# Selective scan: the weighting by C one unit later, in front of the scan

## The chip, the cores and the metric

The kernel runs on one core of a Trainium2 chip. A core has five engines that work through queues of their own, each in order, and that wait for one another through semaphores: TensorE (PE in the profile; its weight loads are PEld), VectorE (DVE), ScalarE (ACT), GpSimd (POOL) and SyncE (SP), which here only issues DMAs. The metric is the device time of one execution in microseconds. The kernel before takes 7552.04 us, the median of three runs (7550.52 to 7557.68).

## The reference

The program is two layers on an image `x` of 2 batches, 128 channels and 64 x 64 places: a deformable convolution with an expert FFN (layer 0), and a Mamba-like mixer with another expert FFN (layer 1). The change touches the selective scan inside the mixer. Per batch it runs over 4096 places with 256 channels and 16 states each:

```python
dA = jnp.exp(jnp.einsum('bdl,dn->lbdn', delta, A))
dBu = jnp.einsum('bdl,bnl,bdl->lbdn', delta, Bm, x)
def step(s, inp):
    a, bu, c = inp
    s = a * s + bu
    return (s, jnp.einsum('bdn,bn->bd', s, c))
_, ys = lax.scan(step, zeros, (dA, dBu, Ct))
y = jnp.transpose(ys, (1, 2, 0))
y = y + x * D[None, :, None]
y = y * silu(z)
out = jnp.einsum('md,bdl->blm', out_proj_w, y)
```

The state of each channel and state number is a running sum over places; at each place the 16 states are weighted by C and added up, x times D is added, the sum is gated by `silu(z)` and projected.

## The kernel before, in words

The scan (`L1Conv.scan`, from line 1568) cuts the work into 512 **units**: 2 batches x 8 pieces of 512 places x 2 halves of the channels x 16 states. A unit has 128 channels on the partitions and 512 places along the row. For unit u the steps are:

- `fetch` (L1615, SyncE): the row of B, broadcast over the partitions, into `bcb`, six units ahead.
- `drive` (L1597, GpSimd): `db` = delta x u times B, three units ahead.
- `decay` (L1604, ScalarE): `da` = exp(delta times A), two units ahead; two slots, so `da` of unit u+2 needs scan(u) finished.
- the scan itself (L1685, VectorE): `h`, 128 x 512; then GpSimd copies the last place into `state` (L1694). Three slots.
- `turn` (L1623, TensorE): four transposes of `h` into `ht` in PSUM, so that the places lie on the partitions. They run in the helper `transpose4`, line 120. Two slots: `ht` of unit u-1 needs that `ht` of unit u-3 has been weighted.
- `weigh` (L1631 on VectorE, L1633 on ScalarE): `w` = `ht` times C, which is now one number per partition. VectorE does all four quarters while there is side work of batch 1 left, later two, and one in batch 1; ScalarE does the others, and its part waits for VectorE's part of the same unit. Four slots.
- `add` (L1639, L1642, TensorE): four transposes back that add `w` onto `py` in PSUM.
- `gate` (L1654, VectorE), once per half: `py` times `zz`, the gated input.

`add` and `gate` wait in a list, `adds`, with the number of the unit in which `flush` issues them.

The order of the work is the order in which the Python loop issues it: every engine's queue holds it in that order. Unit u of the loop issues: DMAs, scan(u), drive(u+3), the state copy, decay(u+2), turn(u-1), weigh(u-2), the adds that are due, and then **other work**. This other work comes from generators that yield after each small step. `side` is the preparation of the next piece (`prepare`, L1484: the taps L1461 or L1434, `px` L1517, `xd` L1520, `ct` L1530, the softplus chain L1540 to L1561 with `e` and `q`) and the projection of the last one (`project`, L1718: matmuls L1727, the residual L1737, its store L1738); it takes two steps per unit. `rest`, only while batch 0 is scanned, is all that batch 1 still has ahead of its own scan: the fuse convolution (L892), the expert FFN of layer 0 in 8 groups (`px` L1045, `ws` L1052, the router L1000 to L1027, `pg` L1032, `po` L1058 and L1061, `xt` L1080) and the patch convolutions (L1251, L1264, L1286, with reductions L1304, L1306, L1343 and L1344 on VectorE). It is paced by a credit of one per unit.

Of the kernel before, what the change touches and what calls it, by code (L numbers as in the profile page):

```python
# [117 lines left out]
def transpose4(nc, ident, ps, srcs):  # L118
    for j, s in enumerate(srcs):
        nc.tensor.transpose(ps[:, j, :], s, ident)  # L120
# [1011 lines left out]
class L1Conv:  # L1132
# [435 lines left out]
    def scan(self, sp, ps, pp, rest, ahead):  # L1568


        env, nc = self.env, self.env.nc
        states = [sp.tile([P, 2, DS], F32, name=f"state{b}", bufs=1) for b in range(B)]
        for state in states:
            nc.vector.memset(state, 0.0)

        dg = sp.tile([P, 2, P], F32, name="dg", bufs=1)
        for h in range(2):
            nc.vector.tensor_scalar(dg[:, h, :], env.ident, self.D[:, h : h + 1], None, ALU.mult)
        NK = N // LC

        def nxt(k):

            res = {}
            return self.prepare(k // NK, k % NK, sp, pp, res), res

        gen, res = nxt(0)
        for _ in gen:
            pass
        units = [(k, half, n) for k in range(B * NK) for half in range(2) for n in range(DS)]
        pieces, das, dbs, rows, hs, hts, ws = {0: res}, {}, {}, {}, {}, {}, {}  # L1590

        def drive(u):

            if u < len(units):
                k, half, n = units[u]
                dbs[u] = sp.tile([P, LC], F32, name="db", bufs=AHEAD + 1)
                nc.gpsimd.tensor_tensor(dbs[u], pieces[k]["du"][:, half, :], rows.pop(u), ALU.mult)  # L1597

        def decay(u):
            if u < len(units):  # L1600
                k, half, n = units[u]
                das[u] = ps.tile([P, LC], F32, name="da")
                dl = pieces[k]["dl"][:, half, :]
                nc.scalar.activation(das[u], dl, AF.Exp, scale=self.A[:, half, n : n + 1])  # L1604

        fetched = 0

        def fetch(u):
            nonlocal fetched
            while fetched <= min(u, len(units) - 1):  # L1610
                k, half, n = units[fetched]
                if "bc" not in pieces.get(k, {}):
                    break
                rows[fetched] = sp.tile([P, LC], F32, name="bcb", bufs=BCB)
                nc.sync.dma_start(out=rows[fetched], in_=pieces[k]["bc"][n].partition_broadcast(P))  # L1615
                fetched += 1

        adds, py = deque(), {}

        def turn(u):  # L1620
            hts[u] = ps.tile([P, GT, P], F32, name="ht")
            h = hs.pop(u)
            transpose4(nc, env.ident, hts[u], [h[:, j * P : (j + 1) * P] for j in range(GT)])  # L1623

        def weigh(u):
            k, half, n = units[u]
            ct, ht = pieces[k]["ct"], hts.pop(u)
            ws[u] = sp.tile([P, GT, P], F32, name="w", bufs=4)
            cut = GT if rest.todo else 2 if k < NK else 1
            by = ct[:, 0:cut, n : n + 1].to_broadcast([P, cut, P])  # L1630
            nc.vector.tensor_tensor(ws[u][:, 0:cut, :], ht[:, 0:cut, :], by, ALU.mult)  # L1631
            for j in range(cut, GT):
                nc.scalar.activation(ws[u][:, j, :], ht[:, j, :], AF.Copy, scale=ct[:, j, n : n + 1])  # L1633

        def add(u):
            k, half, n = units[u]
            if n == 0:
                py[k] = ps.tile([P, LC], F32, name="py", bufs=1)
                nc.tensor.matmul(py[k], dg[:, half, :], pieces[k]["xs"][:, half, :], start=True, stop=False)  # L1639
            w = ws.pop(u)  # L1640
            for j in range(GT):
                nc.tensor.matmul(  # L1642
                    py[k][:, j * P : (j + 1) * P],
                    w[:, j, :],
                    env.ident,
                    is_transpose=True,
                    start=False,
                    stop=n == DS - 1 and j == GT - 1,
                )

        def gate(u):
            k, half, n = units[u]
            y = pieces[k]["zz"][:, half, :]
            nc.vector.tensor_tensor(y, y, py.pop(k), ALU.mult)  # L1654

        def project(k):
            return self.project(k // NK, k % NK, pieces[k]["zz"], sp, pp)

        def flush(u):
            while adds and adds[0][0] <= u:  # L1660
                adds[0][1](adds.popleft()[2])

        fetch(BCB - 3)
        for u in range(AHEAD):
            drive(u)
        decay(0)
        decay(1)
        side, keep, credit = Side(), None, 0
        for u, (k, half, n) in enumerate(units):
            state = states[k // NK]  # L1670
            if k and half == 0 and n == 5:
                side.todo.appendleft(project(k - 1))
            last = n == DS - 4 and half == 1
            if last and k == NK - 1:
                rest.drain()

            if k + 1 < B * NK and k + 1 not in pieces and (k != NK - 1 or not rest.todo):
                gen, pieces[k + 1] = nxt(k + 1)
                side.add(gen)
            fetch(u + BCB - 2)  # L1680
            if k >= NK and u % 24 == 12:
                ahead()

            hs[u] = sp.tile([P, LC], F32, name="h", bufs=3)
            nc.vector.tensor_tensor_scan(  # L1685
                hs[u], das.pop(u), dbs.pop(u), state[:, half, n : n + 1], ALU.mult, ALU.add
            )
            if last:
                side.drain()
                fetch(u + BCB - 2)  # L1690
            drive(u + AHEAD)

            if keep:
                nc.gpsimd.tensor_copy(*keep)  # L1694
            keep = state[:, half, n : n + 1], hs[u][:, LC - 1 : LC]
            decay(u + 2)
            if u:
                turn(u - 1)
            if u > 1:
                weigh(u - 2)  # L1700
            flush(u)
            adds.append((u + (4 if n == 0 else 3), add, u))
            if n == DS - 1:
                adds.append((u + 4, gate, u))

            for _ in range(2 if rest.todo or k != NK - 1 else 4):
                side.step()
            credit += 1
            while credit > 0 and rest.todo:
                credit -= rest.step()  # L1710
        turn(u)
        weigh(u - 1)
        weigh(u)
        flush(u + 4)
        for _ in project(B * NK - 1):
            pass

# [50 lines left out]
class L1Ffn:  # L1768
# [16 lines left out]
    def ahead(self):  # L1785

        if self.early is None:
            self.early = self.ctx.enter_context(self.env.tc.tile_pool(name="f1x", bufs=EARLY, side="right"))
        if len(self.w1) < EARLY:
            self.fetch(self.early)  # L1790
# [325 lines left out]
```

## Time and profile before

| what | value |
|---|---|
| median of three runs | 7552.04 us |
| the profiled execution | 7555.38 us, its span 7553.5 us |
| mean granted TensorE clock | 0.825 |
| busy: PE, DVE, ACT, POOL | 5203.1, 5857.3, 2135.7, 5036.0 us |
| first and last scan (L1685) start | 5764.7 and 7299.4 us |
| scans: count and mean | 512 of 1273 ns |

The scan phase is the last fifth of the program but for the closing FFN of layer 1. In the page's 40 slices it fills numbers 31 to 39. All times in the views are counted from the start of the span. A group's row gives the busy time, the mean of one instruction, and after the bar the idle time of its engine just before it with what ended that idle time.

### The profile page before, as it was taken

The page shows a single profiled execution, that of the slowest core. Times are in us where ns is not written, and L with a number is a line of the kernel's source. Part 1 is how long each engine was busy: PE and PEld are TensorE (multiplying, and loading weights), DVE is VectorE, ACT ScalarE, POOL GpSimd, SP SyncE. Part 2 cuts the span into 40 slices and gives each one's busy share as a digit, 9 for nine tenths or more (in the row PEclk, how much of TensorE's full clock was granted, in tenths as well). Part 3 has the DMA queues.
Part 4 walks back from the last instruction along what each step waited for, and adds up shares of the span by engine and source line. Part 5 has one row for each costly group of instructions (what it writes and reads, how often), then busy time and mean ns, then how long its engine had stood idle before and what let it go on. Part 6 is the DMA issues. An engine that isn't in the chain of part 4 may idle for free.

```text
span 7553.5 us, 71416 instructions
## 1 busy us (share of the span) xinstructions
PE 5203.1 (69%) x22497; PEld 3269.2 (43%) x22497; DVE 5857.3 (78%) x6710; ACT 2135.7 (28%) x4194; POOL 5036.0 (67%) x5062
## 2 busy tenths in 40 slices
PE   4666777777767675766666766666556788867668
PEld 3344444444444442333323444434223567755444
DVE  6878888888888887788888877777775787678782
ACT  2211111111111111311111121211114675667870
POOL 4666777777777777777777776677775445567850
PEclk7887887878888887888888887877777898888899
DMA  7886777776777767877777777687775334555444
GB/s 239 253 275 206 216 210 218 211 220 208 220 213 219 214 210 251 281 232 212 224 217 216 217 232 235 207 251 216 228 208 188 118 103 129 138 155 163 153 148 156
DMA packets 667316, 1550.02 MB, mean 205 GB/s; under 512 B 181668, under 2 KB 230988, under 8 KB 666940
## 3 DMA queue, kind: packets, MB, share of 16 engines
q0 software_dynamic: 307200, 1006.88, 44.2%
q1 hardware_dynamic: 332540, 492.98, 20.9%
q10 hardware_dynamic: 27200, 45.59, 1.6%
q8 instruction: 182, 2.98, 0.2%
q14 instruction: 194, 1.59, 0.1%
HBM read 1436.70 MB, written 110.84 MB: 205 GB/s over the span
## 4 chain that ended last, share of the span: by engine, by line
PE 39%; issue 18%; another core or an unknown queue 13%; DVE 8%; POOL 7%; ACT 7%; DMA 3%; SPq 1%; ACTq 0%; DVEq 0%; POOLq 0%
PE out L816 17%; PE pst L120 6%; POOL v L748 5%; PE po L437 4%; POOL db L1597 2%; DVE h L1685 2%; ACT st L796 2%; DVE v L789 2%; PE ps L1264 2%; PE pfo L892 1%; PE ps L1251 1%; PE px L1045 1%; PE ht L120 1%; DVE q L1557 1%
## 5 line engine op out<-in xcount | busy, mean ns | idle before, releaser
L748 POOL DMA_INDIRECT v<-table,idx x3840 | 4042.1, 1053 | 1629.6 <-issue 1047.7
L789 DVE TENSOR_TENSOR v<-v,pw 128x2048 f32<-128x2048 f32 x960 | 2192.0, 2283 | 611.3 <-DMA v<-table,idx 429.3
L816 PE MATMUL out<-st,regw 128*128 128x512 f32 x3840 | 2234.7, 708 | 225.3 <-issue 164.1
L796 ACT COPY st<-pst 128x512 f32<-128x512 f32 x960 | 556.9, 586 | 4402.2 <-remote 2198.4
L120 PE MATMUL pst<-ident,v 128*128 128x128 f32 x3840 | 721.3, 313 | 1061.0 <-issue 874.3
L791 DVE TENSOR_TENSOR v<-v 128x1024 f32<-128x1024 f32 x960 | 1177.3, 1226 | 33.0
L816 PEld LDWEIGHTS out<-st,regw 128*128 128x128 f32 x3840 | 790.7, 228 | 887.1 <-issue 813.5
L120 PEld LDWEIGHTS pst<-ident,v 128*128 128x128 f32 x3840 | 517.3, 161 | 1431.5 <-issue 1214.8
L1597 POOL TENSOR_TENSOR db<-du,bcb 128x512 f32<-128x512 f32 x512 | 670.9, 1311 | 493.5 <-DVE h L1685 382.8
L1685 DVE TENSOR_TENSOR_SCAN h<-da,state,db 128x512 f32<-128x512 f32 x512 | 651.8, 1273 | 77.9 <-ACT da L1604 48.0
L792 DVE TENSOR_TENSOR v<-v 128x512 f32<-128x512 f32 x960 | 664.2, 692 | 33.0
L120 PE MATMUL ht<-ident,h 128*128 128x128 f32 x2048 | 357.6, 303 | 221.0 <-ACT w L1633 150.9
L437 PE MATMUL po<-wa,win 128*128 128x147 f32 x2112 | 386.4, 306 | 104.7 <-issue 101.9
L437 PEld LDWEIGHTS po<-wa,win 128*128 128x128 f32 x2112 | 339.4, 204 | 226.6 <-issue 226.2
L1604 ACT ACTIVATE da<-delta,w_A_log 128x512 f32<-128x512 f32 x512 | 357.7, 699 | 262.6 <-DVE h L1685 258.0
L120 PEld LDWEIGHTS ht<-ident,h 128*128 128x128 f32 x2048 | 259.8, 155 | 345.4 <-ACT w L1633 223.0
L1631 DVE TENSOR_TENSOR w<-ht,ct 128x128 f32<-128x128 f32 (+2 forms) x512 | 232.8, 455 | 181.9 <-PE ht L120 179.8
L1251 PE MATMUL ps<-ipw,hs 128*120 128x128 f32 x1408 | 212.9, 309 | 181.7 <-ACT X L1198 92.8
L1642 PE MATMUL py<-ident,w 128*128 128x128 f32 x2048 | 337.2, 295 | 0.0
L1251 PEld LDWEIGHTS ps<-ipw,hs 128*120 128x120 f32 x1408 | 196.3, 212 | 235.9 <-ACT X L1198 109.7
L1642 PEld LDWEIGHTS py<-ident,w 128*128 128x128 f32 x2048 | 272.4, 155 | 23.3 <-issue 23.0
L1264 PE MATMUL ps<-tm,X 120*88 120x48 f32 x2048 | 214.9, 278 | 87.2 <-ACT Y L1198 42.2
(327 smaller groups left out, 5289.5 us busy)
## 6 DMA issues: line engine op xcount, KB each, us to landing
bcb<-bc SPq DMA_DIRECT2D x512, 256.0 KB
regw<-in_regw SPq DMA_DIRECT2D x192, 640.0 KB
v<-table,idx POOLq DMA_INDIRECT x3840
yd<-ys ACTq DMA_DIRECT2D x128, 256.0 KB
yc<-yd SPq DMA_DIRECT2D x16, 2048.0 KB
wt<-in_weight SPq DMA_DIRECT2D x32, 1024.0 KB
tm<-pos SPq DMA_DIRECT2D x32, 720.0 KB
pos<-zero SPq DMA_DIRECT2D x48, 240.0 KB
```

What stands on the lines that cost most here:

```text
L120: nc.tensor.transpose(ps[:, j, :], s, ident)
L437: m()
L748: self.env.nc.gpsimd.indirect_dma_start(out=v[:, j, :], out_offset=None, in_=self.table[b], in_offset=bass.IndirectOffsetOnAxis(ap=idx[:, ...
L789: nc.vector.tensor_tensor(v4, v4, w, ALU.mult)
L791: nc.vector.tensor_tensor(up, up, v4[:, :, 2:4, :], ALU.add)
L792: nc.vector.tensor_tensor(v4[:, :, 0, :], v4[:, :, 0, :], v4[:, :, 1, :], ALU.add)
L796: nc.scalar.copy(st, pt.rearrange("p j t -> p (j t)"))
L816: nc.tensor.matmul(self.out[half], self.regw[t // CH][:, t % CH, half * P : (half + 1) * P], st, start=first, stop=last,)
L1251: nc.tensor.matmul(ps[:, k, :], patch, own[o], start=True, stop=True)
L1597: nc.gpsimd.tensor_tensor(dbs[u], pieces[k]["du"][:, half, :], rows.pop(u), ALU.mult)
L1642: nc.tensor.matmul(py[k][:, j * P : (j + 1) * P], w[:, j, :], env.ident, is_transpose=True, start=False, stop=n == DS - 1 and j == GT - 1,)
L1685: nc.vector.tensor_tensor_scan(hs[u], das.pop(u), dbs.pop(u), state[:, half, n : n + 1], ALU.mult, ALU.add)
```

## The change

`weigh` leaves its place behind `turn` and moves to the front of the loop's body, ahead of the scan, for a unit one lower: unit u now issues weigh(u-3), scan(u), and so on, with the other work of the unit still at the end. The unit numbers in `adds` grow by one. The three last units are weighted behind the loop.

```diff
             if k >= NK and u % 24 == 12:
                 ahead()
 
+            if u > 2:
+                weigh(u - 3)
             hs[u] = sp.tile([P, LC], F32, name="h", bufs=3)
             nc.vector.tensor_tensor_scan(
                 hs[u], das.pop(u), dbs.pop(u), state[:, half, n : n + 1], ALU.mult, ALU.add
@@ -1696,12 +1698,10 @@
             decay(u + 2)
             if u:
                 turn(u - 1)
-            if u > 1:
-                weigh(u - 2)
             flush(u)
-            adds.append((u + (4 if n == 0 else 3), add, u))
+            adds.append((u + (5 if n == 0 else 4), add, u))
             if n == DS - 1:
-                adds.append((u + 4, gate, u))
+                adds.append((u + 5, gate, u))
 
@@ -1709,9 +1709,9 @@
         turn(u)
-        weigh(u - 1)
-        weigh(u)
-        flush(u + 4)
+        for i in range(u - 2, u + 1):
+            weigh(i)
+        flush(u + 5)
         for _ in project(B * NK - 1):
             pass
```

## The prediction, as it was put on record

> **What bounds the kernel now.** The profiled execution took 7555.4 us (span 7553.5); the median of the three runs is 7552.0, so it lies 3.3 us above. I read the groups first, to see what one unit costs:
>
> ```profile
> L1685 DVE TENSOR_TENSOR_SCAN h<-da,state,db 128x512 f32<-128x512 f32 x512 | 651.8, 1273 | 77.9 <-ACT da L1604 48.0
> L120 PE MATMUL ht<-ident,h 128*128 128x128 f32 x2048 | 357.6, 303 | 221.0 <-ACT w L1633 150.9
> L1631 DVE TENSOR_TENSOR w<-ht,ct 128x128 f32<-128x128 f32 (+2 forms) x512 | 232.8, 455 | 181.9 <-PE ht L120 179.8
> L1604 ACT ACTIVATE da<-delta,w_A_log 128x512 f32<-128x512 f32 x512 | 357.7, 699 | 262.6 <-DVE h L1685 258.0
> ```
>
> The third line is the change's target: VectorE stands still 180 us in front of `w`, waiting for the transposes `ht`. The scan runs from 5765 to 7300 us only; all before it is untouched. Next came the busy time by stage (PE, PEld, DVE, ACT, POOL; beside it the fuse convolution, the FFN, the patch convolutions, the change of batch, then batch 1 alone):
>
> ```profile
> 5765.00:5893.00 128.00, 100.55 (x424) 57.98 (x424) 91.63 (x132) 96.03 (x134) 70.60 (x86) 0.91 0.60 210
> 5893.00:6200.00 307.00, 245.13 (x1236) 168.34 (x1237) 245.44 (x489) 210.90 (x423) 127.91 (x152) 0.85 0.29 91
> 6200.00:6666.00 466.00, 384.38 (x3087) 344.32 (x3086) 333.28 (x355) 263.56 (x448) 249.24 (x303) 0.86 0.53 143
> 6666.00:6740.00 74.00, 52.76 (x278) 37.74 (x276) 55.75 (x69) 52.80 (x113) 50.57 (x65) 0.79 0.41 131
> 6740.00:7300.00 560.00, 406.23 (x2399) 299.00 (x2400) 449.07 (x586) 461.69 (x1139) 452.13 (x567) 0.86 0.49 158
> ```
>
> TensorE is busiest in the convolutions (384 of 466 us); in the FFN it and VectorE are equal (245 of 307); with batch 1 alone VectorE, ScalarE and GpSimd are level at 80 to 82%, each waiting in turn for another. So no stage is one engine's, and what counts is which wait is lengthened.
>
> **What moves.** Call R the other work that a unit issues. VectorE's order is now scan(u), w(u-2), R(u), scan(u+1), w(u-1); it becomes scan(u), R(u), w(u-2), scan(u+1). That is a rotation: where R is empty nothing moves. In the timeline VectorE has an R in 181 of the 512 units; in the other 331 its order stays. GpSimd's and SyncE's queues keep their order, but SyncE's DMAs after L1738 wait for R. On ScalarE the part of `w` done there passes R too. On TensorE each `add` moves one unit back; the `add` matmuls (L1642) waited 0.0 us, slots of `w` (4) stay as far apart, and gating follows its last `add` by one unit as before: at nothing. If that cover went, one `add` (4 x 0.11 us issue) would show. The tail gains one `add`, 0.4 us.
>
> Three things follow from the rotation.
>
> (a) **Stalls filled.** Where `w` now waits for `ht` and an R stands behind it, R fills the wait, at most min(wait, R). Going through the timeline unit by unit: 47 of 133 stalls have an R behind them. The overlaps sum by stage to 3.7 (fuse), 0.7 (FFN), 19.7 (convolutions), 2.1, and 8.7 us (batch 1). The clearest:
>
> ```profile
> 6900.40 0.29 DVE L1631 TENSOR_TENSOR w<-ht,ct 128x128 f32<-128x128 f32 x1 [1.07 <-PE ht L120]
> 6900.60 0.68 DVE L1737 TENSOR_TENSOR xr<-xr,po 128x512 f32<-128x512 f32 x1
> 6901.31 0.32 SPq L1738 DMA_DIRECT2D x<-xr  x1
> 6902.20 0.41 SPq L1504 DMA_DIRECT2D zc<-zsd  x1
> ```
>
> L1737 (0.68 us) waits behind a `w` that waits 1.07 us, and SyncE's queue behind L1738: in front of `w` it ends some 0.7 us earlier, and the loads behind L1738 with it. This recurs in all 8 pieces of batch 1: -5.5 us, which I take whole. In the convolutions I take half (-10), since TensorE, which VectorE awaits there, is the fuller engine; of the fuse stage half (-2).
>
> (b) **Waits uncovered.** Where R itself waits, `w` stood in front of it and cost nothing; behind it, it adds its 0.67 us (0.27 in batch 1). The sums of min(w, wait of R) are 1.5, 12.3, 3.4, 1.1 and 4.7 us. The FFN's:
>
> ```profile
> 6058.68 1.28 DVE L1685 TENSOR_TENSOR_SCAN h<-da,state,db 128x512 f32<-128x512 f32 x1
> 6059.29 0.60 PE L120 MATMUL ht<-ident,h 128*128 128x128 f32 x4
> 6059.87 0.67 DVE L1631 TENSOR_TENSOR w<-ht,ct 128x512 f32<-128x512 f32 x1
> 6061.95 1.02 PE L1045 MATMUL px<-ew,xnt 128*128 128x512 f32 x2
> 6063.01 0.69 DVE L1052 TENSOR_TENSOR ws<-px,gate 128x512 f32<-128x512 f32 x1 [1.69 <-PE px L1045]
> ```
>
> `w` ends at 6060.5, then L1052 waits 1.69 us for `px`. Some such matmuls themselves wait for an R that now comes 0.67 us sooner, so I take 7 of 12.3 in the FFN, 3 of the convolutions' 3.4, 1 at the change of batch; batch 1's is within (d).
>
> (c) **TensorE held longer.** `ht(u-1)` needs the slot that w(u-3) frees. That `w` used to stand before R(u-1), and now stands behind it, right before scan(u). So I compared the start of every `ht(u-1)` with that of scan(u): in 65 units TensorE was there first, by 3.7, 37.2, 57.3, 11.7 and 25.1 us in sum. Behind a held `ht` stand its `add` and the unit's own matmuls. Not all of it is lost, since TensorE often waits later anyway. Worked through: `ht` at 6051.71 would start near 6053.7, and pushes L1639, L1642, L1058, two L1061 groups and `px` 2.0 us back, onto the L1052 above: 2.0 lost. The group from 5991.02 idles 2.58 us before L1032 and loses 0.2; that from 6147.95 idles 5.72 there and loses about 0.5. Eight such groups at about 1: +8. In the convolutions four bursts of VectorE (at 6267, 6303, 6540, 6640 us) hold it 5.9 to 10.7 us each, mostly idle before as well: 2, 0.7, 1.8 and 1: +5.5.
>
> (d) **ScalarE in batch 1.** Its part of `w` (three copies, 0.88 us) falls behind `xd`, which waits for `px`:
>
> ```profile
> 6924.28 0.91 ACT L1633 ACTIVATE w<-ht,ct 128x128 f32<-128x128 f32 x3
> 6926.88 0.58 ACT L1520 COPY xd<-px 40x512 f32<-40x512 f32 x1 [1.69 <-PE px L1517]
> 6935.56 1.43 DVE L1547 TENSOR_SCALAR q<-e 128x1024 f32<-128x1024 f32 x1 [0.71 <-ACT e L1545]
> ```
>
> Then come the 0.88 us of `w`, da, `ht`, `pt`, `ct`, all in one row up to `e`, for which VectorE already waits 0.71 us: about +1.1 a piece, 8.8 in all. After the q chain (L1547 to L1561) one more `ht` and `add` remain to be done before the chain of scans goes on, about 0.5 a piece: +4.
>
> Sum by stage: fuse -2; FFN +7 +8 = +15; convolutions -10 +3 +5.5 = -1.5; change of batch +1; batch 1 -5.5 +8.8 +4 = +7; tail +0.4. Together **+20 us**: 7575.4 for the profiled execution, and **7572** against the median. Bounds: all of (a) and nothing else, -35 (7517); all uncovered waits (23.0), 15 groups and bursts at the dearest 2.0 us (30) and 1.8 a piece in batch 1 (14), +67 (7619).
>
> A rule bears on (c), apart from this sum. Rows first: the four `ht` took 0.60 us at 6059.29 but 1.11 us at 6922.48 after 6.39 us of idling, and the 16 L1061 took 1.97 us at 6055.02 but 3.67 at 5996.00. The Trainium skill, "TensorE: Matmul & The Clock Gate", Part 1, says that an idle window of some 3.4 us halves TensorE's clock until it has been busy as long; each wait that newly passes that length would cost about 1.7 us (an estimate from that page). Ten of the 65 holds in (c) are that long, so by the rule the sum would be about 17 us higher; I leave it out, since TensorE idled near most of them before.
>
> **The rivals.**
>
> *Faster.* The circle scan, da, ScalarE's copies, TensorE's matmuls, `ht`, `w`, scan in the convolutions may be bound by its latency and not by TensorE. Then all 19.7 us of overlap there are gained, and what (c) and (d) hold back is made up for: -2 -20 -5.5 +7 (FFN, uncovered waits) = -20, 7532. It decides if the convolutions' 96 us of waits of `w` fall below about 80 with the stage shorter by as much. For it: 59 of the 133 stalls lie there. Against: TensorE is 82% busy and most of those stalls (64 of 96 us) have no R behind them. Chance 0.14.
>
> *No change.* From R to R the interval holds one scan and one `w` in both orders; if the moved waits all cancel, the time stays within 15 us (0.2% of 7552, about what a measurement of this kernel can tell from no change). That is also the case in which the change doesn't do what it says, since 331 units keep their order. 7552, chance 0.26.
>
> *Much slower.* The halved clock or longer holds raise (c) to its bound: about 7600. Chance 0.12, beside 0.48 for my own case; together 0.60 for slower.
>
> The range: below 7538 lie the faster cases (0.14), above 7604 about 0.07.
>
> **What would show it.** Right: waits of `w` for `ht` fall from 180 us by 30 to 60 and the total still doesn't fall; waits of `ht` for `w` on VectorE grow (10.4 us in the FFN, 33.1 in the convolutions now); the FFN stage is the longer by 10 to 20 us; L1737 no longer stands behind a stalled `w`; in batch 1 `q` waits longer for `e` than 0.71 us. Wrong: the FFN stage keeps its 307 us, or the convolutions lose more than 10. What would overturn the prediction most is (c): if TensorE's held matmuls are made up for everywhere, the time is 7552 or less.

## The result, and the profile after

The changed kernel took 7578.24 us (median of 8 runs, 7570.08 to 7599.68) against 7552.87 us (7543.96 to 7562.25) for the kernel before in the same rounds: the ratio is 1.003 with a 95% interval of 1.0021 to 1.0038, so it is slower by some 25 us. The execution that was profiled took 7599.68 us (span 7597.9), the longest of the eight, 21 us above the median. So its stage times overstate the loss: the five stages below come to 38 us more than before, and another 6.5 us lie ahead of the first scan, where the two programs are the same.

The groups of after, which answer to the four shown of before:

```profile
L1687 DVE TENSOR_TENSOR_SCAN h<-da,state,db 128x512 f32<-128x512 f32 x512 | 652.2, 1274 | 43.0 <-ACT da L1604 19.8
L120 PE MATMUL ht<-ident,h 128*128 128x128 f32 x2048 | 371.6, 311 | 269.6 <-ACT w L1633 170.7
L1631 DVE TENSOR_TENSOR w<-ht,ct 128x128 f32<-128x128 f32 (+2 forms) x512 | 235.8, 461 | 198.9 <-PE ht L120 182.2
L1604 ACT ACTIVATE da<-delta,w_A_log 128x512 f32<-128x512 f32 x512 | 358.9, 702 | 221.6 <-DVE h L1687 214.2
```

The scan itself no longer stands still 78 us but 43 us. That is no gain: the idle time in front of `w` rose from 182 to 199 us (what it waits for `ht` only from 180 to 182), and that of TensorE in front of `ht` from 221 to 270 us. The waits have changed places.

The busy time by stage (PE, PEld, DVE, ACT, POOL), cut at the starts of the same scans (units 0, 36, 100, 227, 256 and 511):

```profile
5771.20:5900.50 129.30, 102.59 (x423) 59.18 (x424) 92.92 (x131) 95.99 (x134) 72.68 (x86) 0.90 0.60 209
5900.50:6218.10 317.60, 251.78 (x1232) 171.37 (x1231) 256.33 (x490) 212.14 (x424) 133.78 (x153) 0.83 0.27 87
6218.10:6694.40 476.30, 392.80 (x3089) 350.86 (x3088) 339.25 (x355) 264.74 (x449) 258.43 (x304) 0.85 0.51 140
6694.40:6774.30 79.90, 54.05 (x282) 39.55 (x282) 55.22 (x70) 53.31 (x114) 51.96 (x67) 0.79 0.39 124
6774.30:7344.20 569.90, 426.89 (x2395) 310.43 (x2392) 452.14 (x584) 465.80 (x1136) 457.10 (x565) 0.84 0.47 154
```

Between the same scans the kernel before takes 128.9, 307.6, 466.2, 73.3 and 558.8 us. Three things are to be seen. Every stage is longer, the first by 0.4 us only. In the FFN VectorE is busy 256 us, where between the same scans it was 246 before with the same work (490 instructions): some of its own instructions have become longer. And the change of batch, 80 us long, loses 6.6 us.

**The FFN, held transposes.** The timeline of after at the same place as the prediction's example (units 68 to 73):

```profile
6066.49 0.68 DVE L1631 TENSOR_TENSOR w<-ht,ct 128x512 f32<-128x512 f32 x1
6067.23 0.42 PEld L120 LDWEIGHTS ht<-ident,h 128*128 128x128 f32 x4 [2.67 <-DVE w L1631]
...
6078.43 1.02 PE L1045 MATMUL px<-ew,xnt 128*128 128x512 f32 x2
6079.49 0.69 DVE L1052 TENSOR_TENSOR ws<-px,gate 128x512 f32<-128x512 f32 x1 [4.12 <-PE px L1045]
6080.10 0.68 DVE L1631 TENSOR_TENSOR w<-ht,ct 128x512 f32<-128x512 f32 x1
```

TensorE waits 2.67 us in front of `ht` until the `w` behind the router has run, its queue moves back, `px` comes late, and L1052 waits 4.12 us where it waited 1.69. `w` then stands behind that wait. From scan 69 to scan 73 it is 21.1 us, before 17.8.

Not all of these 3.3 us is the hold itself. Measured from scan 68, `ht` starts 2.1 us later than before. But the matmuls that come behind the wait also take longer: L1058 1.41 us (before 1.12), and the 16 of L1061 3.30 us (before 1.97), together 1.6 us. The trace grants TensorE half the clock for 3.41 us from 6068.52 on, behind 2.5 us of idling for `w`; in the kernel before it is the full clock from 6046 to 6058.

```profile
6055.02 1.97 PE L1061 MATMUL po<-ident,ws 128*128 128x128 f32 x16
```

```profile
6069.15 3.30 PE L1061 MATMUL po<-ident,ws 128*128 128x128 f32 x16
```

**The FFN, longer instructions.** The other finding is in the same timeline. First before, then after:

```profile
6059.87 0.67 DVE L1631 TENSOR_TENSOR w<-ht,ct 128x512 f32<-128x512 f32 x1
6060.04 1.27 POOL L1597 TENSOR_TENSOR db<-du,bcb 128x512 f32<-128x512 f32 x1 [3.65 <-DVE h L1685]
6060.66 0.67 DVE L99 SCALAR_TENSOR_TENSOR n_nb<-n_mv,n_rs 128x4 f32<-128x4 f32 x1
```

```profile
6074.09 1.27 POOL L1597 TENSOR_TENSOR db<-du,bcb 128x512 f32<-128x512 f32 x1 [4.25 <-DVE n_rs L84]
6074.11 1.26 DVE L99 SCALAR_TENSOR_TENSOR n_nb<-n_mv,n_rs 128x4 f32<-128x4 f32 x1
```

L99 works on 4 elements per partition and takes 0.16 us when GpSimd is idle. Here it ends in both kernels within 0.1 us of GpSimd's `db`: it has waited inside itself for GpSimd. `db` starts when the scan has ended. Before, `w` stood there, ran beside `db` at its usual 0.67 us, and L99 waited only for the rest. After, L99 stands there and waits for all of `db`; `w` comes behind it. The rows of the FFN stage, before and after:

```profile
L99 DVE SCALAR_TENSOR_TENSOR n_nb<-n_mv,n_rs 128x4 f32<-128x4 f32 x16 | 6.2, 388 | 0.5
L1010 DVE TENSOR_TENSOR lg<-lg,s 128x32 f32<-128x32 f32 x8 | 3.5, 439 | 0.3
L1549 DVE TENSOR_TENSOR q<-q,e 128x1024 f32<-128x1024 f32 x2 | 2.5, 1226 | 0.1
```

```profile
L99 DVE SCALAR_TENSOR_TENSOR n_nb<-n_mv,n_rs 128x4 f32<-128x4 f32 x16 | 12.8, 799 | 0.5
L1010 DVE TENSOR_TENSOR lg<-lg,s 128x32 f32<-128x32 f32 x8 | 6.2, 778 | 0.3
L1549 DVE TENSOR_TENSOR q<-q,e 128x1024 f32<-128x1024 f32 x2 | 4.4, 2182 | 0.1
```

L99 has grown by 6.6 us, L1010 by 2.7 and L1549 by 1.9; a few others became shorter, by less than 3 us each. No row of idle time shows this, since the instruction counts as busy. The Trainium skill, "SBUF — State Buffer", section "SBUF: two separate sides", says that GpSimd's SBUF ports are VectorE's second pair, held as an exclusive lock for a whole instruction, and that a VectorE instruction with two SBUF inputs needs the pair against a GpSimd instruction that reads SBUF. The rows agree: L99 and L1010 have two inputs in SBUF, and where they are long they end within 0.06 us of a GpSimd instruction, mostly `db`; `w`, with one input in PSUM, keeps its 0.67 us beside it.

**The change of batch.** Before, then after:

```profile
6682.93 0.69 DVE L1737 TENSOR_TENSOR xr<-xr,po 128x512 f32<-128x512 f32 x1 [8.23 <-DMA xr<-x]
6683.54 1.28 DVE L1685 TENSOR_TENSOR_SCAN h<-da,state,db 128x512 f32<-128x512 f32 x1
```

```profile
6712.23 0.69 DVE L1737 TENSOR_TENSOR xr<-xr,po 128x512 f32<-128x512 f32 x1 [10.26 <-DMA xr<-x]
6712.84 0.42 DVE L1631 TENSOR_TENSOR w<-ht,ct 128x256 f32<-128x256 f32 x1
...
6713.37 0.63 ACT L1633 ACTIVATE w<-ht,ct 128x128 f32<-128x128 f32 x2 [9.47 <-DVE w L1631]
6714.05 1.12 PE L120 MATMUL ht<-ident,h 128*128 128x128 f32 x4 [5.61 <-ACT w L1633]
...
6720.51 0.42 DVE L1631 TENSOR_TENSOR w<-ht,ct 128x256 f32<-128x256 f32 x1 [3.05 <-PE ht L120]
```

One instruction waits for a load, L1737. Before, the `w` of the unit had run; now it waits behind L1737, ScalarE's part of it too (9.47 us), and TensorE's next transposes (5.61 us). When the load has come, the scan goes on, but TensorE has transposes and side work to make up for, and `w` waits 3.05 us. The wait for the load is also 2.0 us longer. In both kernels the load is issued 3.4 us after the `po` matmuls (L1727) start and ends L1737's wait 5.0 us later; but those matmuls now start 1.9 us after VectorE has come to stand at L1737, and before they started 0.2 us ahead of that. From scan 230 to scan 235 the place loses 3.8 us; the rest of the 6.6 us arises at other units, 1.8 of it at unit 228, where the gate waits 1.07 us for `py`.

**Batch 1.** L1737 at unit 7 of a piece:

```profile
7008.87 0.29 DVE L1631 TENSOR_TENSOR w<-ht,ct 128x128 f32<-128x128 f32 x1 [0.48 <-PE py L1642]
7009.08 1.27 DVE L1687 TENSOR_TENSOR_SCAN h<-da,state,db 128x512 f32<-128x512 f32 x1
7011.09 0.69 DVE L1737 TENSOR_TENSOR xr<-xr,po 128x512 f32<-128x512 f32 x1 [0.74 <-PE po L1727]
7011.70 0.28 DVE L1631 TENSOR_TENSOR w<-ht,ct 128x128 f32<-128x128 f32 x1
```

As predicted, it no longer stands behind a stalled `w`; but it now waits 0.74 us itself, for `po`. And there is a wait that the kernel before did not have: `w` for `py` (0.48 us), that is for a slot of `w` which a later `add` frees. The gate, L1654, has a new one as well:

```profile
7043.06 0.29 DVE L1631 TENSOR_TENSOR w<-ht,ct 128x128 f32<-128x128 f32 x1 [1.07 <-PE ht L120]
7043.27 1.27 DVE L1687 TENSOR_TENSOR_SCAN h<-da,state,db 128x512 f32<-128x512 f32 x1
...
7046.21 0.69 DVE L1654 TENSOR_TENSOR zc<-zc,py 128x512 f32<-128x512 f32 x1 [1.67 <-PE py L1642]
7046.81 0.28 DVE L1631 TENSOR_TENSOR w<-ht,ct 128x128 f32<-128x128 f32 x1
```

### The profile page after: what moved, and what is told of

It is laid out like the page before. It is cut to its first block, busy times and chain, and to the rows that moved or that the text cites. A ratio compares the mean times of both kernels' runs of the same rounds, so it can differ in the third digit from the quotient of the medians.

```text
span 7597.9 us, 71447 instructions
## 1 busy us (share of the span) xinstructions
PE 5232.3 (69%) x22497; PEld 3299.8 (43%) x22497; DVE 5880.6 (77%) x6710; ACT 2146.8 (28%) x4196; POOL 5093.7 (67%) x5062
## 5 line engine op out<-in xcount | busy, mean ns | idle before, releaser
L1597 POOL TENSOR_TENSOR db<-du,bcb 128x512 f32<-128x512 f32 x512 | 694.6, 1357 | 516.8 <-DVE h L1687 340.5
L1251 PE MATMUL ps<-ipw,hs 128*120 128x128 f32 x1408 | 211.3, 307 | 152.4 <-ACT X L1198 72.9
L1264 PE MATMUL ps<-tm,X 120*88 120x48 f32 x2048 | 224.9, 284 | 68.7 <-ACT Y L1198 38.5
```

Source lines behind the costliest of these rows:

```text
L1251: nc.tensor.matmul(ps[:, k, :], patch, own[o], start=True, stop=True)
```

## The experiments

The runs from e1 on were made on three chips, on which the kernel before took 7562.4 us (e1, e2, e5, e6), 7508.4 us (e4, e8, e9) and 7217.9 us (e7, e10, e11, e13); each ratio is against the kernel before on the same chip. The first two rows are the pair of the result; its chip is not recorded. Differences of a few us between stage times are no more than the spread: without the rotation and the late adds beside it, the FFN took 303.3 to 308.0 us in five profiles (before, e2, e8, e9, e13). The stage times are differences of scan starts in the one profiled execution of each kernel. "Rotation" is `w` in front of the scan, "late" the adds and the gate one unit later; b0 and b1 are the batches.

| run | rotation | late | FFN | patch conv. | change | batch 1 | ratio (95%) |
|---|---|---|---|---|---|---|---|
| before | - | - | 307.6 | 466.2 | 73.3 | 558.8 | 1 |
| after | all | all | 317.5 | 476.3 | 79.9 | 569.9 | 1.0030 (1.0021-1.0038) |
| e1_batch0 | b0 | b0 | 317.3 | 468.4 | 79.7 | 564.2 | 1.0025 (1.0015-1.0035) |
| e2_batch1 | b1 | b1 | 305.9 | 467.8 | 73.8 | 568.4 | 1.0013 (1.0003-1.0022) |
| e5_adds_stay | all | - | 319.6 | 465.7 | 79.1 | 561.9 | 1.0032 (1.0020-1.0044) |
| e6_adds_late | - | all | 300.2 | 464.3 | 73.8 | 571.0 | 1.0002 (0.9993-1.0010) |
| e7_late_b0 | - | b0 | 302.7 | 463.2 | 72.3 | 559.7 | 0.9985 (0.9976-0.9994) |
| e8_late_b1 | - | b1 | 308.0 | 466.3 | 73.2 | 572.9 | 1.0011 (1.0000-1.0021) |
| e9_late_b1_w5 | - | b1 | 306.5 | 470.6 | 74.3 | 573.9 | 1.0017 (1.0008-1.0026) |
| e10_gate_far | all | gate, first adds | 316.6 | 473.0 | 81.1 | 578.9 | 1.0059 (1.0046-1.0072) |
| e11_pick | 2 of 32 units, b1 | b0 | 301.5 | 463.9 | 72.9 | 558.1 | 0.9985 (0.9976-0.9993) |
| e13_conv_only | patch conv. | - | 303.3 | 468.1 | 73.8 | 563.1 | 1.0004 (0.9993-1.0014) |
| e4_ht3_before | - | - | 313.4 | 509.2 | 92.2 | 720.9 | 1.0333 (1.0318-1.0349) |
| e4_ht3_after | all | all | 314.6 | 506.7 | 94.1 | 714.1 | 1.0326 (1.0309-1.0342) |

The theory after the first reading: the rotation makes the loss, by held transposes and uncovered waits, as predicted. The rival: the late adds make it, by the new waits for `py`.

### One batch alone

```diff
 e1, against the changed kernel (weigh and late adds in the new order where front holds):
+        front = lambda u: u < 256        # e2: u >= 256
...
-            if u > 2:
-                weigh(u - 3)
+            while weighed < u - 2:
+                weigh(weighed)
+                weighed += 1
...
             if u:
                 turn(u - 1)
+            while weighed < u - 1 and not front(u + 1):
+                weigh(weighed)
+                weighed += 1
             flush(u)
+            late = 1 if front(u + 2) or front(u + 3) else 0
-            adds.append((u + (5 if n == 0 else 4), add, u))
+            adds.append((u + late + (4 if n == 0 else 3), add, u))
...
```

> The new order in units 0 to 255 (batch 0, beside the fuse convolution, FFN, patch convolutions and change of batch), the old one in 256 to 511. Theory (rotation: uncovered waits and held transposes, as predicted, plus what the profile after added): batch 0 carries the larger part of the loss, +10 to +20 us, the FFN stage 8 to 12 longer, the patch convolutions up to 10 longer. Rival (late adds, new waits of w and of the gate on py, 16 us of them in batch 0 and 16 in batch 1): half of the loss, +10 to +14. Rival (batch 1's ScalarE): about 0.

> The new order in units 256 to 511 only. Theory: +7 to +11 us, all of it in the 8 pieces of batch 1 at about 1 to 1.4 us a piece; the stages of batch 0 keep their times within the noise of a profile. Rival (batch 1 is a chain from scan to scan that the rotation leaves alone): 0. With e1 the two parts should add up to the whole, +25 us; if they add up to much less, the order at the change of batch or a coupling of the stages matters.

Measured: 1.0025 and 1.0013, in sum the whole within the intervals. The losses appear mostly where the new order is: e1 loses 18.7 us in batch 0 and e2 9.6 in batch 1. Batch 1 of e1 is 5.4 us longer than before, though its order there is the old one; so is that of e13, which takes 563.1 us, so this is spread. Batch 0 carries two thirds.

### The rotation alone, the late adds alone

```diff
 e5, against the changed kernel:
-            adds.append((u + (5 if n == 0 else 4), add, u))
+            adds.append((u + (4 if n == 0 else 3), add, u))
             if n == DS - 1:
-                adds.append((u + 5, gate, u))
+                adds.append((u + 4, gate, u))
 e6, against the kernel before: the same lines the other way round
```

> The rotation on VectorE as in the changed kernel, but the add matmuls and the gating stay in the unit that they have in the kernel before (TensorE's order is that of the kernel before). Theory (rotation alone makes the loss): as the changed kernel, 7570 to 7585, or longer, since an add now follows its w more closely on TensorE and can wait for it: waits of py for w, 0.0 us so far, would show. Rival (the late adds make the loss, by the waits of w and gate on py): 7550 to 7560, and the waits of w for py, 15 us in the changed kernel, are gone.

> The kernel before with only the add matmuls and the gating one unit later; the weighting stays behind the scan. Theory (adds were free, matmul waits of 0.0 us): 7550 to 7558. Rival (late adds make the loss): +13 to +25, that is 7566 to 7578, with waits of w and of the gate for py (8 and 8 us in the patch convolutions, 5 and 11 in batch 1 of the changed kernel) present here as well.

The rotation alone has the whole loss (1.0032), the late adds alone none that can be measured (1.0002). The rival falls for the total. But the stages of e6 show that its zero is a sum of two: batch 1 is 12 us longer than before, batch 0 shorter. And in e5 batch 1 hardly loses. So in batch 1 it is the late adds that cost, and the rotation costs in batch 0 (e5 18.9 us there, e1 with late adds 18.7). e7 and e8 test the late adds.

### Late adds in one batch

```diff
 e7, against the kernel before:
-            adds.append((u + (4 if n == 0 else 3), add, u))
+            late = 1 if u < 256 else 0        # e8: u >= 256
+            adds.append((u + late + (4 if n == 0 else 3), add, u))
             if n == DS - 1:
-                adds.append((u + 4, gate, u))
+                adds.append((u + late + 4, gate, u))
```

> The kernel before with the add matmuls and the gating one unit later in units 0 to 255 only. With it the two halves of the run with late adds alone stand apart (late in batch 1 alone measured 1.0011). Theory (late adds cost batch 1 only; beside the FFN they free TensorE a little: 300 us there against 306 to 308 elsewhere): FFN stage 299 to 303, the whole 0 to -7 us (1.0000 to 0.9990). Rival (the 300 us were the spread of a profile): FFN 305 to 309, the whole 0.

> The kernel before with the add matmuls and the gating one unit later in units 256 to 511 only; the weighting stays behind the scan. In the profiles so far batch 1 took 568 to 571 us wherever adds were late there and 559 to 564 wherever not, in either order. Theory (in batch 1 the late adds make the loss, by w of four units later, whose slot the late first add of a half frees): batch 1 at 568 to 572, the whole +5 to +10. Rival (the difference is that of two profiles): 559 to 565, the whole 0.

The signs came out as the theory had them: 1.0011 for batch 1 and 0.9985 for batch 0. e7 gained more than expected, 11 us in the whole where 0 to 7 were named. All profiles agree on batch 1: it takes 568 to 574 us in the five kernels with all adds late there (after, e2, e6, e8, e9), 579 with the first adds and the gate late (e10), and 558 to 564 in the six without (before, e1, e5, e7, e11, e13), in either order. In batch 0 the sum of the four stages is 966.2 to 967.7 us with late adds and the old order (e6, e7, e11), and 976.0 to 976.8 without either (before, e2, e8). Of these e6 ran on the first chip and e7 and e11 on the third. With the rotation the late adds show no such gain: batch 0 takes 994.6 us in e1 and 994.8 in e5. Where in batch 0 the gain arises, and why, stays open: e13, on the third chip and with the old adds, has an FFN of 303.3 us, hardly longer than the 302.7 of e7.

### Where batch 1 loses: the slot of w, or the gate

```diff
 e9, against e8:
-BCB = 8
+BCB = 7
-            ws[u] = sp.tile([P, GT, P], F32, name="w", bufs=4)
+            ws[u] = sp.tile([P, GT, P], F32, name="w", bufs=5)
 e10, against the changed kernel:
-            adds.append((u + (5 if n == 0 else 4), add, u))
+            adds.append((u + (5 if n == 0 else 3), add, u))
```

> The former run with 5 slots of w (and 7 of the broadcast rows, to make room). Theory (the slot of w is what the late adds cost): waits of w for py, 10 us in batch 1, are gone, and batch 1 is back at 559 to 565, the whole 0 to +3. Rival (late adds cost something else, such as the gating behind them): as the former run.

> The changed order of the weighting, with the adds in the unit that they have in the kernel before (the first add of a half as in the changed kernel), but the gating as late as in the changed kernel, so two units behind its last add instead of one. Theory (in batch 1 the loss is the gate's wait for its last add, 10 to 11 us, with w and the scan now behind it): waits of zc for py in batch 1 fall from 10.9 below 3 us, units 19 to 22 of a piece take 12.0 us or less instead of 13.1, batch 1 takes 556 to 563 us instead of 570; the whole 1.0015 to 1.0025, since the FFN and the change of batch keep their loss of 12 and 6. Rival (the stop only moves to the next w or the q chain): batch 1 at 567 to 572, the whole 1.003.

Neither theory held. In e9 the waits of `w` for `py` are gone (10.1 us in e8) and batch 1 takes 573.9 us as in e8; but the waits of `db` for its broadcast rows rose there from 11.7 to 51.9 us, since those had a slot less, so the slot is not cleared either. In e10 the gate no longer waits, as the timeline at the place shown above has it, and the time is worse, 1.0059:

```profile
6697.80 0.29 DVE L1631 TENSOR_TENSOR w<-ht,ct 128x128 f32<-128x128 f32 x1 [1.07 <-PE ht L120]
6698.01 1.27 DVE L1687 TENSOR_TENSOR_SCAN h<-da,state,db 128x512 f32<-128x512 f32 x1
6699.20 0.66 DVE L1654 TENSOR_TENSOR zc<-zc,py 128x512 f32<-128x512 f32 x1
...
6702.47 1.11 DVE L1547 TENSOR_SCALAR q<-e 128x1024 f32<-128x1024 f32 x1 [0.79 <-ACT e L1545]
...
6708.36 0.29 DVE L1631 TENSOR_TENSOR w<-ht,ct 128x128 f32<-128x128 f32 x1 [0.86 <-PE py L1642]
```

The gate's 1.67 us are back behind it, as waits for `e` and `py` (and 0.34 for `ht` between). That the longest new wait is the price was only an argument, and it fell: units 19 to 23 of a piece take 17.8 us with this gate and 17.9 with the other, against 16.8 before. The waits of e5 say the same: without late adds the gate waits 10.2 us for `py` in batch 1, nearly as in the changed kernel (10.9), and batch 1 is only 3 us longer than before. Why e10 loses a further 1.0 us in units 3 to 7 of a piece was not followed.

What can be said is where the loss lies. The mean time of stretches of a piece in batch 1 (us, over the first seven pieces; the last has no next piece to prepare):

| units of the piece | before | e5 rotation | e8 late | after | e10 |
|---|---|---|---|---|---|
| 3 to 7 | 9.2 | 9.1 | 9.8 | 9.6 | 10.6 |
| 8 to 14 | 14.7 | 14.5 | 14.8 | 14.5 | 14.6 |
| 19 to 23 | 16.8 | 17.6 | 17.6 | 17.9 | 17.8 |
| 24 to 31 | 14.8 | 14.6 | 14.8 | 14.6 | 14.6 |

Of the units left out, 0 to 2 take 4.2 us in all five kernels and 15 to 18 from 13.7 to 14.1. With the old order late adds cost in two stretches, each of which holds the first add of a half (with the two `dg` matmuls L1639) and the gate of the half before. In units 3 to 7 only the kernels lose that have both of these a unit later, so the runs do not tell which of the two costs, nor by which of its followers. In units 19 to 23, where the softplus chain is, the rotation alone loses 0.8 us too, and gets more than half of it back elsewhere; with the late adds on top (after) the stretch is hardly longer than with either.

### Three slots for the transposes

```diff
 e4_ht3_after, against the changed kernel; e4_ht3_before, the same against the kernel before:
-                das[u] = ps.tile([P, LC], F32, name="da")
+                das[u] = sp.tile([P, LC], F32, name="da")
...
-            hts[u] = ps.tile([P, GT, P], F32, name="ht")
+            hts[u] = ps.tile([P, GT, P], F32, name="ht", bufs=3)
...
-BCB = 8
+BCB = 6
```

> The changed order with three PSUM slots for the transposes ht instead of two; the two slots of da move to SBUF for it, and the broadcast rows get 6 slots instead of 8, to make room. To be read against its twin with the order of before. Theory (held transposes, step c, make the FFN's loss): waits of ht for w on VectorE in the FFN fall from 96 us (40.9 and 54.7) below 50, and the FFN stage is at most 4 us longer than the twin's; the whole at most 12 us longer than the twin. Rival (uncovered waits, step b: w behind waits of L1052): the FFN stage stays 8 to 12 us longer than the twin's, the whole 20 to 25.

> The order of before, with the same three slots of ht, da in SBUF and 6 slots of broadcast rows. It is the twin by which the former run is read. By both theories within 30 us of the kernel before; fewer waits of ht for w may make it faster, and dearer reads of da or later broadcast rows slower.

Both kernels are 3.3% (some 250 us) slower than the kernel before, where 30 us at most were expected: the 512 scans, which now read `da` from SBUF, are 266 us longer in sum (1792 ns in the mean, not 1273). As a pair they still answer the question. With three slots the order costs nothing: 7753.16 against 7760.31 us, with overlapping intervals. In the FFN 0.5 us of waits of `ht` for `w` are left with the old order and none with the new, and the stage differs by 1.2 us, not 10; the change of batch differs by 1.9, not 6.6. The FFN windows, first of the old order, then of the new:

```profile
5869.30:6182.70 313.40, 242.85 (x1249) 165.95 (x1248) 255.85 (x489) 211.78 (x423) 139.12 (x152) 0.86 0.28 91
```

```profile
5868.90:6183.60 314.70, 247.88 (x1238) 171.50 (x1237) 262.06 (x490) 212.20 (x424) 143.37 (x152) 0.83 0.29 90
```

VectorE is 6.2 us longer busy here too, the third figure: the lock against GpSimd does not depend on the slots. But the stage hardly grows, for the waits of L1052 for `px` shrink by as much:

```profile
DVE ws L1052 <- PE px L1045: 38.0, 16, 8.3
```

```profile
DVE ws L1052 <- PE px L1045: 32.3, 16, 6.2
```

With two slots they grew instead (38.5 us before), and TensorE waits for `w`. The weight loads of `ht` wait 54.7 us, before 11.7, and its matmuls 40.9, before 7.6; the two rows overlap, and with the overlap counted once it is 60.7 us against 11.7:

```profile
PEld ht L120 <- DVE w L1631: 54.7, 40, 4.7
DVE ws L1052 <- PE px L1045: 41.2, 18, 7.1
PE ht L120 <- DVE w L1631: 40.9, 25, 4.5
```

So the held transposes are needed for the FFN's loss, with one reserve: the circle of the scan is slower in this pair (batch 1 takes over 710 us), which can hide small losses; the FFN stage, at 313 us, is close to that of the kernel before. Whether the lengthened instructions or the slower matmuls cost anything of their own with two slots was not tried; the former do lengthen the holds, since they stand in front of `w`.

### The convolutions alone

```diff
+        front = lambda u: 100 <= u < 227
```

(the rest as in e1, with `late = 0`)

> The new order in units 100 to 226 only (beside the patch convolutions), adds and gating as before. The step of the prediction that took -10 us of filled stalls there, +8.5 of new waits, is tested alone. Theory (the stage's bound is TensorE, so neither counts): the stage at 464 to 469 us, the whole 0.9995 to 1.0005. The rival of the prediction (latency bounds the circle, 20 us of stalls are filled): stage at 450 to 455, the whole 0.998. The other side (as the profile of the changed kernel had it): stage at 476, the whole 1.0013.

1.0004, and the stage takes 468.1 us: neither the predicted gain of filled stalls nor the 10 us that the profile of the changed kernel lost (the interval of the whole alone would still allow these). The waits of `w` for `ht` did fall, from 96.1 to 77.0 us, and the stage was not shorter for it, so the rival that called the circle bound by its latency falls. With the new order the stage takes 465.7 to 476.3 us in five profiles, without 463.2 to 470.6 in seven: in the mean 4 us longer, hardly more than the spread.

### A version that beats both

```diff
+        front = lambda u: u >= 256 and u % 32 in (8, 13)
...
+            late = 1 if u < 256 else 0
```

> A version meant to beat both: the order of before, adds and gating one unit later in batch 0 only, and the new order in batch 1 only in units 8 and 13 of a piece, where it fills a stall with the work of the unit before (L1737 and the one after). Theory: in the pieces of batch 1, unit 7 takes 2.8 us instead of 3.15 and unit 12 3.4 to 3.8 instead of 4.13, batch 1 2 to 8 us shorter; the FFN up to 6 shorter; the whole 0.9985 to 0.9995. Rival (what unit 12 gains is lost again in units 10 to 14): 1.0000.

0.9985, faster than both, but no faster than e7 with late adds in batch 0 alone. Against the kernel before the two units gained as expected (unit 7 of a piece takes 2.76 us, not 3.14; unit 12 takes 3.34, not 4.13, over seven pieces), and units 10, 11 and 13 gave back 1.0 (unit 14 gained 0.4): batch 1 is 558.1 us, in e7 559.7. That 1.6 us is below what these runs tell apart. What is shown is the gain of e7, moving the adds and the gate back in batch 0 without touching `w`.

## Why the prediction was right or wrong

The total was right: 7572 predicted, 7578 measured, slower by 25 us where 20 were forecast. Of the four parts of its working one was right, (c), and the closeness of the total is in good part luck.

- **What moves.** Right that the rotation alone sets the sign: e5 has the whole loss. "Slots of `w` (4) stay as far apart, gating follows its last `add` by one unit as before: at nothing" was wrong in batch 1, where late adds cost 8 to 14 us in either order, and right in sum. With the old order they gain about 10 us in batch 0 as well; with the new one e1 and e5 show no gain there, and the whole still comes out alike (e5 1.0032, after 1.0030).
- **(a) Stalls filled.** In the convolutions -10 was taken. The waits of `w` for `ht` there did fall by 17, from 96 to 79 us, but 15 us of new waits for `py` (by `w` 8.1, by the gate 7.1) came and VectorE was busy 6 us longer. In e13, with the adds of before, the waits fell by 19 us, and the stage gained nothing either. In batch 1 L1737 came out from behind `w`, and waited for `po` instead: unit 7 is 0.32 us shorter, half of the 0.7, some 2.5 us in 8 pieces where 5.5 were taken whole.
- **(b) Waits uncovered.** 7 us were taken for the FFN. With three slots, where only (b) and the lengthened instructions are left, the order costs 1.2 us in all. As far as that pair stands for two slots, this term was too large. At the change of batch it was too small, +1 for 6 to 8 measured (after, e1, e5, e10): the price was taken as at most the length of one `w`, but behind the `w` at L1737 stood ScalarE's part and TensorE's queue for the 9 to 10 us of one load, and this place alone lost 3.8 us. That is read from the timeline; no run moves this `w` alone.
- **(c) TensorE held longer.** Right in mechanism: waits of `ht` for `w` in the FFN rose from 11.7 to 60.7 us, in the example `ht` came 2.1 us later where 2.0 were worked out, and three slots take the FFN's loss away. +8 was taken; the stage lost 10 in the profile of after and 9 to 12 in e1, e5 and e10, of which 1.2 remain with three slots. What the term lacked are the 10 us by which VectorE's own instructions grow, and the matmuls that took 1.6 us longer behind the example's wait, so that it lost 3.3 us.
- **(d) ScalarE in batch 1.** Wrong. `xd` does wait longer for `px` (16.1 to 22.9 us in sum), but `q` waits less for `e`, not more (6.1 us in sum before, 4.7 in e5), so the row up to `e` did not carry the delay on, and the rotation without late adds leaves batch 1 at 561.9 us, inside the range of the kernels without it. The 8.8 + 4 that were taken here agree by chance with the 10 us of the late adds.
- **The sum by stage**: fuse -2 (measured +0.4), FFN +15 (+9.9), convolutions -1.5 (+10.1 in that profile, +4 in the mean), change of batch +1 (+6.6), batch 1 +7 (+11.1). Errors of both signs met; and these stages, of the slowest execution, come to 38 us where the medians differ by 25.
- **The clock.** For batch 1 it was rightly left out: e8 and e11 have the same granted clock there (0.85) and the same busy time of TensorE, and lie 15 us apart (rows below, first e8, then e11). In the FFN it was more than nothing, though e5 speaks against its being the main part. In the example it makes 1.6 of the 3.3 us. With the rotation alone (e5) the stage's granted clock is 0.85 as before, TensorE is busy only 3 us longer, and the stage loses 12; in after the clock is 0.83 and TensorE is busy 6 us longer. With three slots the clock falls from 0.86 to 0.83, with 5 us more busy time, and the stage loses 1.2; so slower matmuls alone need not cost, and what they add to the holds no run separates. The count of ten holds of 3.4 us was no good measure: in the scan phase of after the clock is halved 48 times, and in 9 of them only had TensorE been idle for the whole 3.4 us before; in half of them it had been busy for 32% of that time or more.

```profile
6687.50:7260.40 572.90, 408.06 (x2391) 297.31 (x2389) 449.36 (x584) 462.86 (x1136) 454.65 (x564) 0.85 0.50 154
```

```profile
6381.60:6939.70 558.10, 408.43 (x2399) 301.79 (x2396) 450.96 (x585) 463.14 (x1136) 454.98 (x565) 0.85 0.48 158
```

- **What would show it.** That waits of `w` for `ht` fall by 30 to 60 us was wrong (180 before, 182 after), and so was the longer wait of `q` for `e`. Longer waits of `ht` came true, and so did L1737; the FFN's 9.9 us (9 to 12 in e1, e5 and e10) lie at the lower edge of the 10 to 20 named. The sign that would have told against it, convolutions losing more than 10, stood in the profile of after (10.1); the other four profiles with the new order lose 7 us or less, one of them nothing.

## What to carry to other kernels

In a queue that runs in order, an instruction whose result frees a slot for another engine belongs in front of whatever may wait, even if it stalls itself: here the order costs nothing once there is a third slot, and a `w` behind one slow load cost some 4 us. Look also at what runs on GpSimd at the place to which an instruction of VectorE moves: here `w`, which reads PSUM, kept its 0.67 us beside GpSimd's `db`, and L99, with two inputs in SBUF, grew from 0.16 us to as much as 1.27. And when a change moves two things, take each alone and by stage: with the old order the measured zero of the late adds was a gain and a loss of about 10 us each, and the gain alone made the faster kernel.

## What the runs showed of the hardware

- VectorE and GpSimd: in the FFN stage of after, L99 took 1.18 us in the mean in the 10 cases that began while `db` was running (0.16 in the other 6), and ended within 0.06 us of it each time; L1010 took 0.97 us in the 6 cases that began while GpSimd ran `db` or another instruction, again ending within 0.06 us of it, and 0.19 in the other 2.
- The scan with `da` in SBUF instead of PSUM took 1792 ns in the mean, not 1273. In e4_ht3_before the 118 scans with no GpSimd instruction beside them took 1275 ns, and the 371 that began while one was running 1986 ns in the mean; in the kernel before, with `da` in PSUM, the 347 that began beside one took 1273 ns and the 139 with none 1274. This fits the same lock, since the scan then has two inputs in SBUF, and it is the price of e4:

```profile
L1685 DVE TENSOR_TENSOR_SCAN h<-da,state,db 128x512 f32<-128x512 f32 x512 | 917.7, 1792 | 143.1 <-POOL state L1694 115.3
```

- The chip matters more than the change: the same kernel took 7562, 7508 and 7218 us on three chips. On the third the granted clock was 0.861 (e7), on the first 0.826 (e1); the part ahead of the scan was shorter by 350 us (first scan at 5419.5 against 5769.4 us), the scan of batch 1 by only 4.5.
